# Float32 pair products as three one-pass products of 12-bit parts, with the bank scaled between the second and the third

## The chip, the cores and the metric

One core of one Trainium2 chip. The metric is the device time of one execution in microseconds (us), as the median of several runs; lower is better. Engines are named as in the profile: PE is TensorE, PEld its weight loads, DVE VectorE, ACT ScalarE, POOL GpSimd. A "pair" is one of the 496 products below; a "bank tile" is its 128 x 1024 float32 result in PSUM.

## The reference

32 fields of 128 numbers for 1024 rows; for each of the 496 pairs of fields i < j, field i is multiplied by the pair's own 128 x 128 matrix and then elementwise by field j:

```python
v_i = inputs[:, I_IDX, :]
v_j = inputs[:, J_IDX, :]
transformed = jnp.einsum('bpd,ped->bpe', v_i, W)   # float32
return transformed * v_j                            # 1024 x 496 x 128
```

The check of results passes kernels whose products are off by about one part in 4000. So "correct" below doesn't tell the precision of two variants apart.

## The kernel before

x is held in SBUF transposed (128 x 1024 a field), the weights stream in chunks of 8 pairs. A pair is two float32 matmuls of 512 columns into one bank tile, then VectorE multiplies by field j into an output tile of two pairs, which a DMA takes away.

```python
for q, (i, j) in enumerate(pairs):
    # ... loads of weight chunk q // WC + 3 and of field j + 3 on ScalarE's queue
    po = ppool.tile([P, BT], F32, tag="po", name=f"po_{q}")          # 4 buffers, all of PSUM
    for h in range(0, BT, HB):                                        # BT = 1024, HB = 512
        nc.tensor.matmul(po[:, h : h + HB], w_sb[q // WC][:, q % WC, :],
                         x_sb[i][:, h : h + HB], start=True, stop=True)
    r = q % OC
    if r == 0:
        ot = opool.tile([P, OC, BT], F32, tag="ot", name=f"ot_{q}")
    # ... the last pairs are cut in halves
    nc.vector.tensor_tensor(ot[:, r, :], po[:, :], x_sb[j][:, :], ALU.mult)
    if r == OC - 1:
        nc.sync.dma_start(out=out_v[:, q - r : q + 1, :], in_=ot[:, :, :])
```

## Time and profile before

| what | value |
|---|---|
| time | 877.84 us, median of 3 (877.59 to 878.51); 877.8 to 878.6 beside each later group of runs |
| TensorE | busy 98%, 1984 records of 0.432 us each: 1.72 us a pair |
| VectorE | busy 69%, 1.225 us a pair |
| ScalarE, GpSimd | no arithmetic |
| DMA | 309.7 MB; 418 to 420 GB/s while x still loads, 343 to 351 after that |

A busy line gives the summed busy time, its share of the span and the number of instructions. A line of the costliest groups gives source line, engine, operation, output <- inputs, shape and count, then busy us and mean ns, then the engine's idle time just before those instructions and what ended it. A timeline line gives start, length, and how many instructions in a row it joins. The ends of matmuls are modelled, so I read spacing from the starts, not from the lengths. The lines themselves are in the prediction.

### The profile page before, as it was taken

What the parts mean: (1) busy time and instruction counts of PE and PEld (TensorE: products, weight loads), DVE (VectorE), ACT (ScalarE), POOL (GpSimd) and SP (SyncE); (2) the same over time, 40 slices, a digit from 0 to 9 for tenths busy, and PEclk for the clock granted to TensorE, in tenths of its full rate; (3) what the DMA queues carried; (4) which work ended last, traced back from release to release, by engine and by line L of the source; (5) the groups of instructions that cost most, each with busy time, mean ns of one, the idle gap of its engine ahead of it and who ended that gap; (6) DMA issues with size and microseconds to landing.
All of it is one profiled execution on the core that took longest, in us unless ns stands there. A gap on an engine that the chain in (4) does not pass through costs nothing.

```text
span 876.1 us, 5490 instructions
## 1 busy us (share of the span) xinstructions
PE 856.6 (98%) x1984; PEld 377.1 (43%) x1984; DVE 606.3 (69%) x498; POOL 0.2 (0%) x4
## 2 busy tenths in 40 slices
PE   8997899999999999999999999999999999999997
PEld 3432344444444444444444444444444444444443
DVE  4744677777777777777777777777777777777775
POOL 0000000000000000000000000000000000000000
PEclk9999999999999999999999999999999999999999
DMA  9999999989898898998988889888898989889877
GB/s 349 421 419 421 421 420 415 357 340 354 333 352 342 338 357 333 349 339 341 353 340 346 339 346 352 339 345 339 351 343 341 346 338 355 342 338 351 329 311 296
DMA packets 81898, 309.69 MB, mean 353 GB/s; under 512 B 5584, under 2 KB 5840, under 8 KB 81872
## 3 DMA queue, kind: packets, MB, share of 16 engines
q1 hardware_dynamic: 68624, 262.16, 75.3%
q10 hardware_dynamic: 13248, 47.19, 15.5%
q8 instruction: 15, 0.25, 0.1%
q14 instruction: 11, 0.09, 0.0%
HBM read 49.28 MB, written 260.05 MB: 353 GB/s over the span
## 4 chain that ended last, share of the span: by engine, by line
PE 88%; DMA 11%; DVE 0%; ACTq 0%; DVEq 0%; issue 0%; SPq 0%
PE po L82 88%; DMA x<-in_xt_dram 6%; DMA out_dram<-ot 3%; DMA w<-in_wt_dram 2%; DVE ot L93 0%; DVE ot L99 0%; DVEq L121 0%; ACTq L61 0%; ACTq L53 0%; DVEq L93 0%; SPq L95 0%
## 5 line engine op out<-in xcount | busy, mean ns | idle before, releaser
L82 PE MATMUL po<-x,w 128*128 128x512 f32 x1984 | 856.6, 594 | 13.9 <-DVE ot L93 9.9
L93 DVE TENSOR_TENSOR ot<-po,x 128x1024 f32<-128x1024 f32 x494 | 603.7, 1225 | 264.7 <-PE po L82 228.1
L82 PEld LDWEIGHTS po<-x,w 128*128 128x128 f32 x1984 | 377.1, 190 | 492.6 <-issue 470.0
L99 DVE TENSOR_TENSOR ot<-po,x 128x512 f32<-128x512 f32 x4 | 2.6, 687 | 0.9 <-PE po L82 0.9
L115 POOL MEMSET const-bfloat16-1.0<- 128x1 bf16 x1 | 0.1, 102 | 0.0
L115 POOL MEMSET const-uint8-127<- 128x1 uint8 x1 | 0.1, 102 | 0.0
L115 POOL MEMSET const-float32-0.0<- 128x1 f32 x1 | 0.1, 99 | 0.2 <-issue 0.2
L115 POOL MEMSET const-float32-1.0<- 128x1 f32 x1 | 0.1, 99 | 0.0
## 6 DMA issues: line engine op xcount, KB each, us to landing
out_dram<-ot SPq DMA_DIRECT2D x247, 1024.0 KB, 4.8
w<-in_wt_dram ACTq DMA_DIRECT2D x61, 512.0 KB, 4.3
x<-in_xt_dram ACTq DMA_DIRECT2D x28, 512.0 KB, 12.8
x<-in_xt_dram SPq DMA_DIRECT2D x4, 256.0 KB, 4.6
x<-in_xt_dram SPq DMA_DIRECT2D x2, 512.0 KB, 8.5
out_dram<-ot SPq DMA_DIRECT2D x4, 256.0 KB, 3.3
w<-in_wt_dram ACTq DMA_DIRECT2D x1, 320.0 KB, 6.3
w<-in_wt_dram ACTq DMA_DIRECT2D x1, 128.0 KB, 3.6
```

The costliest lines, as they stand in the source:

```text
L82: nc.tensor.matmul(po[:, h : h + HB], w_sb[q // WC][:, q % WC, :], x_sb[i][:, h : h + HB], start=True, stop=True,)
L93: nc.vector.tensor_tensor(ot[:, r, :], po[:, :], x_sb[j][:, :], ALU.mult)
L99: nc.vector.tensor_tensor(ot[:, r, s], po[:, s], x_sb[j][:, s], ALU.mult)
L115: nc = _bacc.Bacc("TRN2", target_bir_lowering=False, num_devices=1)
```

## The change

The intent: by the Trainium skill, "FP8 and Floating Point Precision", TensorE Precision Notes, a float32 product passes the array four times, and reduced-precision float32 is cut to a short format; I took float32r for that type, and to pass once. Split both operands into an upper and a lower part of 12 bits: w = wh + wl, x = xh + e xl, with e = 2^-12. Four part products are then needed, but Karatsuba's identity makes three of them do, all accumulated in one bank:

    (1 + e) (wh xh + wl xl) + (wl - e wh)(xh - xl) = (wh + wl)(xh + e xl)

The first two products (called F, four matmuls of 512 columns) go in; ScalarE scales the bank by 1 + e in PSUM; the third (S, two matmuls) is added. ScalarE also rounds the upper parts, GpSimd makes the lower parts and the differences. The pairs are walked in another order so that x can load as it goes; the first 15 pairs stay float32. The core of the diff:

```diff
-WC = 8
-OC = 2
+WC = 4
+EPS = 2.0**-12
+NATIVE = 5
+LAG = 2
...
-    return [(i, j) for j in range(1, NF) for i in range(j)]
+    return [(i, j) for i in range(NF - 2, -1, -1) for j in range(i + 1, NF)]
...
+    def split_w(c):
+        raw = w_raw[c].rearrange("p q e -> p (q e)")
+        h, l, d = [wpool.tile([P, WC * P], F32R, tag=t, name=f"{t}_{c}") for t in ("wh", "wl", "wd")]
+        hs = tpool.tile([P, WC * P], F32, tag="t", name=f"whs_{c}")
+        nc.scalar.mul(h, raw, 1.0 - 2.0**-13)
+        nc.gpsimd.tensor_tensor(l, raw, h.bitcast(F32), ALU.subtract)
+        nc.gpsimd.tensor_scalar(hs, h.bitcast(F32), EPS, 1.0, ALU.mult, ALU.mult)
+        nc.gpsimd.tensor_tensor(d, l.bitcast(F32), hs, ALU.subtract)
+    # ... split_x(f): the same for one field, in two halves of 512 columns
...
+    def second(q):
+        r = slice(q % WC * P, (q % WC + 1) * P)
+        for h in range(0, BT, HB):
+            nc.tensor.matmul(po[q][:, h : h + HB], w_s[q // WC][2][:, r], x_s[i][2][:, h : h + HB],
+                             start=False, stop=True, skip_group_check=True)
+    for q in range(NQ + LAG):
+        # ... loads, split_w two chunks ahead, split_x one field ahead
+        # ... the first 15 pairs: two float32 matmuls, as before; all others:
+        for t in (0, 1):
+            for h in range(0, BT, HB):
+                nc.tensor.matmul(po[q][:, h : h + HB], w_s[c][t][:, r], x_s[i][t][:, h : h + HB],
+                                 start=t == 0, stop=t == 1)
+        nc.scalar.mul(po[q], po[q], 1.0 + EPS)
+        if q >= LAG:
+            second(q - LAG)      # where q - LAG is a split pair
+            finish(q - LAG)      # VectorE's product and the output DMA
```

The source puts S of a pair two pairs after its F. The program that was built has another order, as the prediction says.

More of the change, by code (lines that the diff above doesn't have):

```diff
@@ L8 @@
 F32 = mybir.dt.float32
+F32R = mybir.dt.float32r
 ALU = mybir.AluOpType
@@ L40 @@
     pairs = _pairs()
+    nchunk = NQ // WC
     xpool = ctx.enter_context(tc.tile_pool(name="x", bufs=1))
-    wpool = ctx.enter_context(tc.tile_pool(name="w", bufs=4))
+    spool = ctx.enter_context(tc.tile_pool(name="xs", bufs=2))
+    rpool = ctx.enter_context(tc.tile_pool(name="wr", bufs=4))
+    wpool = ctx.enter_context(tc.tile_pool(name="ws", bufs=3))
+    tpool = ctx.enter_context(tc.tile_pool(name="tmp", bufs=2))
     opool = ctx.enter_context(tc.tile_pool(name="o", bufs=6))
@@ L47, with load_x @@
     x_sb = {}
-    def load_x(f, eng, pieces=1):
+    def load_x(f, pieces=1):
         x_sb[f] = xpool.tile([P, BT], F32, tag=f"x{f}", name=f"x_{f}")
@@ L52, in load_x @@
         for k in range(pieces):
-            eng.dma_start(out=x_sb[f][:, k * s : (k + 1) * s], in_=xt[:, f, k * s : (k + 1) * s])
-    nchunk = NQ // WC
-    w_sb = {}
+            nc.sync.dma_start(out=x_sb[f][:, k * s : (k + 1) * s], in_=xt[:, f, k * s : (k + 1) * s])
+    w_raw = {}
     def load_w(c, splits=(0, WC)):
-        w_sb[c] = wpool.tile([P, WC, P], F32, tag="w", name=f"w_{c}")
+        w_raw[c] = rpool.tile([P, WC, P], F32, tag="w", name=f"w_{c}")
         for a, b in zip(splits, splits[1:]):
-            nc.scalar.dma_start(out=w_sb[c][:, a:b, :], in_=wt[:, c * WC + a : c * WC + b, :])
@@ L63 @@
-    load_w(0, (0, 1, 3, WC))
-    load_x(0, nc.sync, 2)
-    load_x(1, nc.sync, 2)
-    load_x(2, nc.sync)
+            nc.sync.dma_start(out=w_raw[c][:, a:b, :], in_=wt[:, c * WC + a : c * WC + b, :])
+    w_s = {}
+    def split_w(c):
[6 more added lines that the diff above has]
+        nc.gpsimd.tensor_tensor(d, l.bitcast(F32), hs, ALU.subtract)
+        w_s[c] = (h, l, d)
@@ new lines, with split_x @@
+    x_s = {}
+    def split_x(f):
+        h, l, d = [spool.tile([P, BT], F32R, tag=t, name=f"{t}_{f}") for t in ("xh", "xl", "xd")]
+        for a in range(0, BT, HB):
+            s = slice(a, a + HB)
+            ls = tpool.tile([P, HB], F32, tag="t", name=f"xls_{f}_{a}")
+            nc.scalar.mul(h[:, s], x_sb[f][:, s], 1.0 - 2.0**-13)
+            nc.gpsimd.tensor_tensor(ls, x_sb[f][:, s], h[:, s].bitcast(F32), ALU.subtract)
+            nc.gpsimd.tensor_scalar(l[:, s], ls, 1.0 / EPS, 1.0, ALU.mult, ALU.mult)
+            nc.gpsimd.tensor_tensor(d[:, s], h[:, s].bitcast(F32), l[:, s].bitcast(F32), ALU.subtract)
+        x_s[f] = (h, l, d)
@@ L67 @@
+    nq0 = NATIVE * (NATIVE + 1) // 2
+    c0 = nq0 // WC
+    load_w(0, (0, 1, WC))
+    load_x(NF - 2, 2)
+    load_x(NF - 1, 2)
+    load_x(NF - 3)
     load_w(1)
-    load_x(3, nc.sync)
+    for f in (NF - 4, NF - 5):
+        load_x(f)
     load_w(2)
-    load_x(4, nc.scalar)
-    load_x(5, nc.scalar)
-    out_v = out.rearrange("q e b -> e q b")
-    ot = None
-    for q, (i, j) in enumerate(pairs):
-        if q % WC == 0 and q // WC + 3 < nchunk:
-            load_w(q // WC + 3)
-        if i == 0 and 5 < j + 3 < NF:
-            load_x(j + 3, nc.scalar)
-        po = ppool.tile([P, BT], F32, tag="po", name=f"po_{q}")
+    out_v = out.rearrange("q e b -> q e b")
@@ new lines, with finish @@
+    po = {}
+    def finish(q):
+        j = pairs[q][1]
+        ot = opool.tile([P, BT], F32, tag="ot", name=f"ot_{q}")
+        pieces = 2 if q >= NQ - 2 else 1
+        s0 = BT // pieces
+        for k in range(pieces):
+            s = slice(k * s0, (k + 1) * s0)
+            nc.vector.tensor_tensor(ot[:, s], po[q][:, s], x_sb[j][:, s], ALU.mult)
+            nc.sync.dma_start(out=out_v[q, :, s], in_=ot[:, s])
+    def second(q):
+        i, _ = pairs[q]
+        r = slice(q % WC * P, (q % WC + 1) * P)
@@ L81 @@
         for h in range(0, BT, HB):
             nc.tensor.matmul(
-                po[:, h : h + HB],
-                w_sb[q // WC][:, q % WC, :],
-                x_sb[i][:, h : h + HB],
-                start=True,
-                stop=True,
-            )
-        r = q % OC
-        if r == 0:
-            ot = opool.tile([P, OC, BT], F32, tag="ot", name=f"ot_{q}")
-        if q < NQ - OC:
-            nc.vector.tensor_tensor(ot[:, r, :], po[:, :], x_sb[j][:, :], ALU.mult)
-            if r == OC - 1:
-                nc.sync.dma_start(out=out_v[:, q - r : q + 1, :], in_=ot[:, :, :])
-        else:
-            for h in range(0, BT, HB):
-                s = slice(h, h + HB)
-                nc.vector.tensor_tensor(ot[:, r, s], po[:, s], x_sb[j][:, s], ALU.mult)
-                nc.sync.dma_start(out=out_v[:, q, s], in_=ot[:, r, s])
+                po[q][:, h : h + HB], w_s[q // WC][2][:, r], x_s[i][2][:, h : h + HB], start=False, stop=True,
@@ new lines, in second @@
+                skip_group_check=True,
+            )
+    for q in range(NQ + LAG):
+        if q < NQ:
+            i, j = pairs[q]
+            c = q // WC
+            if q % WC == 0:
+                if c + 3 < nchunk:
+                    load_w(c + 3)
+                for k in ([c + 2] if c > 0 else [0, 1, 2]):
+                    if c0 <= k < nchunk:
+                        split_w(k)
+            if j == i + 1:
+                for f in ([i - 4] if i < NF - 2 else [NF - 6]):
+                    if f >= 0:
+                        load_x(f)
+                if 0 <= i - 1 < NF - 1 - NATIVE:
+                    split_x(i - 1)
+            po[q] = ppool.tile([P, BT], F32, tag="po", name=f"po_{q}")
+            if q < nq0:
+                for h in range(0, BT, HB):
+                    nc.tensor.matmul(
+                        po[q][:, h : h + HB],
+                        w_raw[c][:, q % WC, :],
+                        x_sb[i][:, h : h + HB],
+                        start=True,
+                        stop=True,
+                    )
+            else:
+                r = slice(q % WC * P, (q % WC + 1) * P)
+                for t in (0, 1):
+                    for h in range(0, BT, HB):
+                        nc.tensor.matmul(
+                            po[q][:, h : h + HB],
+                            w_s[c][t][:, r],
+                            x_s[i][t][:, h : h + HB],
+                            start=t == 0,
+                            stop=t == 1,
+                        )
+                nc.scalar.mul(po[q], po[q], 1.0 + EPS)
+        if q >= LAG:
+            if q - LAG >= nq0:
+                second(q - LAG)
+            finish(q - LAG)
```

## The prediction

> **What bounds the kernel now.** I read the page first (busy shares, chain, costliest groups), then a table of stretches for the load by stage, then timelines of TensorE. The lines of the page:
>
> ```profile
> PE 856.6 (98%) x1984; PEld 377.1 (43%) x1984; DVE 606.3 (69%) x498; POOL 0.2 (0%) x4
> ...
> PE po L82 88%; DMA x<-in_xt_dram 6%; DMA out_dram<-ot 3%; DMA w<-in_wt_dram 2%; DVE ot L93 0%; DVE ot L99 0%; DVEq L121 0%; ACTq L61 0%; ACTq L53 0%; DVEq L93 0%; SPq L95 0%
> ...
> L82 PE MATMUL po<-x,w 128*128 128x512 f32 x1984 | 856.6, 594 | 13.9 <-DVE ot L93 9.9
> L93 DVE TENSOR_TENSOR ot<-po,x 128x1024 f32<-128x1024 f32 x494 | 603.7, 1225 | 264.7 <-PE po L82 228.1
> ```
>
> The chain of work that ended last is TensorE for 88%. There are 496 pairs and 1984 matmul records, four to a pair (two for each half of 512 columns). 856.6/1984 = 0.432 us each, so a pair costs 1.72 us of TensorE. VectorE needs 1.225 us a pair and waits 228 us for TensorE: it has room. Two stretches of the table (columns: us, busy PE, PEld, DVE, POOL with counts, clock, DMA share, GB/s):
>
> ```profile
> 22.00:44.00 22.00, 22.00 (x53) 9.80 (x52) 15.90 (x13) 0.00 (x0) 1.00 1.03 420
> 400.00:500.00 100.00, 100.00 (x235) 44.27 (x234) 71.34 (x59) 0.00 (x0) 1.00 0.89 343
> ```
>
> From 22 to 150 us, while x is still being loaded, the DMA engines give 418 to 420 GB/s at a share of 1.02 to 1.03: this is their ceiling. Later TensorE is always busy and DMA moves 343 to 351. So the kernel is TensorE bound with DMA close behind. The timeline of TensorE in the saturated stage shows what restarting costs:
>
> ```profile
> 68.60 3.70 PE L82 MATMUL po<-x,w 128*128 128x512 f32 x8 [1.08 <-DVE ot L93]
> 73.48 3.70 PE L82 MATMUL po<-x,w 128*128 128x512 f32 x8 [1.18 <-DVE ot L93]
> ```
>
> Eight matmuls without a stop would be 7 x 0.429 + 0.592 = 3.59 us; after a wait they take 3.70, so each wait of TensorE costs about 0.11 us more (the weights' load is then not hidden).
>
> **What the Trainium skill says.** (1) "FP8 and Floating Point Precision", TensorE Precision Notes: true FP32 is four passes through the array, reduced-precision FP32 reads four bytes and is cut to a shorter format. The trace agrees with four if one record is two passes. (2) "TensorE: Matmul & The Clock Gate", Back-to-back issue gap: 512 columns warm take 512/2.4 + 2.5 = 216 ns; half of the traced 0.43 us is 0.215, which agrees. No run yet shows a float32r pass, so 0.216 us is an estimate. (3) "ScalarE: Activation LUTs", What ACT_TABLE_LOAD costs: an ACTIVATE with immediates takes 186 ns + 0.833 ns per element, back-to-back ones overlap by 93 ns. ScalarE computes nothing in this trace, so nothing here confirms it. (4) "GPSIMD Engine Reference", Performance versus the Vector engine: tensor_tensor of 2048 fp32 is 4497 ns there, so about 1.12 us for 512 (estimate); one-input operations are near line rate, I take 0.6 us. GpSimd does no such work in this trace.
>
> **The change, part by part.**
>
> *Removed:* for 481 of 496 pairs the four records of 0.43 us. The first 15 stay as they were: 15 x 1.72 = 25.8 us.
>
> *Added on TensorE:* six one-pass matmuls a pair: F = h and l products, 4 x 0.216 = 0.86 us; S = the difference product, 2 x 0.216 = 0.43 us. Sum 1.29 us, 25% less. If only this counted, 481 x 1.29 = 620 us, and DMA would bind: 309.7 MB / 420 GB/s = 737 us.
>
> *Added between F and S:* ScalarE scales the bank in place, A = 186 + 0.833 x 1024 = 1.04 us. S(q) cannot start before A(q) has ended. The source puts S two pairs after F, which would give A(q) 0.43 + 0.86 + 0.43 + 0.86 = 2.58 us. But the order of instructions in the built kernel is another one. In 102 of the 120 groups of four pairs TensorE's queue stands as F0 F1 S0 F2 S1 F3 S2 S3, then F0 of the next group: only F1 stands between F0 and S0, and only S2 between F3 and S3. ScalarE's queue has the split of a weight chunk (512 elements, 0.61 us) between A2 and A3. TensorE's queue is in order, so it waits.
>
> I walk one group, in us from the start of F0, with 0.20 from the end of a matmul's issue to a reader's start (in the trace VectorE starts 0.63 us after its last matmul's start, whose slot is 0.43), 0.04 back to TensorE (the trace restarts it 0.05 after VectorE), and 0.11 for a restart:
> - F0 0 to 0.86; A0 1.06 to 2.10; F1 to 1.72; S0 could go at 1.72 but waits to 2.14, and with the restart runs 2.25 to 2.68.
> - A1 2.01 to 3.05; F2 2.68 to 3.54; S1 follows at once, to 3.97. A2 3.74 to 4.78; F3 3.97 to 4.83; S2 just fits, 4.83 to 5.26.
> - The weight split takes ScalarE from 4.69 to 5.30; A3 5.21 to 6.25; S3 waits from 5.26 to 6.29 and runs 6.40 to 6.83.
>
> So a group takes 6.83 us instead of 5.16: 1.71 us a pair, which is what a pair costs now. The TensorE time saved is given back as two waits for ScalarE in each group. 120.25 groups x 6.83 = 821 us. In 12 boundaries the next F comes ahead of S3, saving both waits (1.14 + 0.53 us): -20 us. Some 11 groups have S directly behind its own F, about +1.3 us each: +14 us. That leaves 815 us.
>
> *Moved or added beside other work:* the weight split on GpSimd is 2 x 1.12 + 0.6 = 2.85 us a chunk, the x split 5.7 us for each i: 121 x 2.85 + 26 x 5.7 = 493 us, off the path with two chunks of lead. ScalarE: 481 x 0.95 + 173 x 0.52 = 547 us. VectorE stays at 1.225 a pair (610 us). All DMA goes through one queue, with w in 2 KB pieces a partition; at 1.71 us a pair output and weights are 0.59 MB / 1.71 = 345 GB/s, as now. The x loads, now early and saturating, spread over the whole run.
>
> *Ends:* first matmul at about 4.5 us, tail as now 876.1 - 870.5 = 5.6 us. Sum: 4.5 + 25.8 + 815 + 5.6 = 851, plus about 2 from span to time: 853 us. I take 848, because the waits for ScalarE may be a little shorter than I walk them, and every 0.05 us there, paid twice in each of 120 groups, is 12 us in all.
>
> **Rivals.**
> 1. *DMA becomes the bound.* If TensorE does not wait as I think, the floor is 737 us at 420 GB/s, and some 750 to 775 us with the ends and 2 KB pieces. For it: the gap between 343 and 420 GB/s is small, and 1.29 us is less than 0.59 MB / 420 GB/s = 1.40 us. Against it: the built order, which puts S too close to F.
> 2. *ScalarE's round trip is longer than I think.* If A with its semaphores is 0.15 us longer, S0 and S3 wait that much more and S1 and S2 begin to wait too, with two more restarts: 120 x (0.30 + 0.15 + 0.35) = +96 us, some 940 us. For it: S2 fits with only 0.01 us in hand. Against it: where S1 and S2 wait, the later waits shrink in part, so less than this.
> 3. *GpSimd becomes the bound in the first groups.* A group of i with n pairs needs 5.7 + 0.71 n us of GpSimd against 1.71 n of TensorE: equal at 6 pairs, the first split group. If its operations are half again as slow, groups up to about 13 pairs are bound by it: some +15 us.
> 4. *A float32r matmul is no faster than one record of now* (0.43 us): 481 x 2.59 = 1246 us. I give it 4%.
>
> **Range and chances.** The walk of one group gives 1.71 us with perhaps 0.09 either way, which is 43 us; DMA cannot let it fall below 750. I say 848 us, 8 times in 10 within 790 to 905. Faster by over 2% is below 860, slower is above 895: 0.61 faster, 0.26 within, 0.13 slower.
>
> **What the changed profile would show.** Right: matmuls of half the spacing (0.215 us); TensorE's largest wait is for the scaling line of ScalarE, about 1.6 us in each group of four pairs, 180 us or so in all, at the S line; scaling records near 1.04 us; DMA around 350 to 370 GB/s with a share below 0.95 in the middle; VectorE idle between pairs. Wrong: DMA at 415 to 420 throughout with VectorE waiting for output buffers (rival 1); S1 and S2 waiting as well (rival 2); waits for GpSimd before 150 us (rival 3); spacing of 0.43 us (rival 4). A clock granted below 1.00 because TensorE has gaps would also upset it.

## The result, and the profile after

| | before | after |
|---|---|---|
| time, median | 878.17 us (877.59 to 878.66, 4 runs) | 897.87 us (897.74 to 899.2, 4 runs) |
| span, granted clock | 876.1 us, 0.998 | 896.0 us, 0.999 |
| TensorE busy | 98% | 85% |
| DMA at 400 to 500 us | 343 GB/s, share 0.89 | 340 GB/s, share 0.90 |

The ratio is 1.0228 (95% interval 1.021 to 1.0246): slower by 2.3%. I had forecast 848 us and faster. The time lies inside my range, the direction is the one that I had given 0.13.

Lines of the page after, from the busy times and the costliest groups:

```profile
PE 761.1 (85%) x2946; PEld 526.2 (59%) x2946; DVE 607.0 (68%) x498; ACT 558.2 (62%) x655; POOL 549.5 (61%) x523
...
L177 ACT ACTIVATE po<-po 128x1024 f32<-128x1024 f32 x481 | 476.9, 1009 | 298.5 <-PE po L170 298.5
L135 PE MATMUL po<-xd,wd 128*128 128x512 f32 x962 | 325.7, 420 | 123.8 <-ACT po L177 123.0
...
L170 PE MATMUL po<-xh,wh 128*128 128x512 f32 x962 | 300.9, 394 | 0.0
L170 PE MATMUL po<-xl,wl 128*128 128x512 f32 x962 | 298.1, 391 | 0.0
L170 PEld LDWEIGHTS po<-xl,wl 128*128 128x128 f32 x962 | 180.6, 188 | 42.2
```

L170 is F, L177 the scaling, L135 is S. No engine is busy for more than 85%, for F no wait is recorded, and S waits 123 us for the scaling. The list of waits (waiter <- releaser: us in total, times, longest) has it on both halves of TensorE, and the table of stretches shows that DMA is no limit (us, busy PE, PEld, DVE, ACT, POOL with counts, clock, DMA share, GB/s):

```profile
PEld po L135 <- ACT po L177: 162.8, 195, 1.7
...
PE po L135 <- ACT po L177: 123.0, 245, 1.2
```

```profile
400.00:500.00 100.00, 84.48 (x333) 59.05 (x333) 67.52 (x57) 63.49 (x74) 59.14 (x57) 1.00 0.90 340
```

One group of four pairs on TensorE's timeline, from S0 (508.14) to the S0 of the next group (515.15):

```profile
508.14 0.70 PE L135 MATMUL po<-xd,wd 128*128 128x512 f32 x2
508.67 0.63 PE L170 MATMUL po<-xh,wh 128*128 128x512 f32 x2
509.14 0.62 PE L170 MATMUL po<-xl,wl 128*128 128x512 f32 x2
509.60 0.62 PE L135 MATMUL po<-xd,wd 128*128 128x512 f32 x2
510.06 0.63 PE L170 MATMUL po<-xh,wh 128*128 128x512 f32 x2
510.52 0.62 PE L170 MATMUL po<-xl,wl 128*128 128x512 f32 x2
510.98 0.63 PE L135 MATMUL po<-xd,wd 128*128 128x512 f32 x2
512.31 0.73 PE L135 MATMUL po<-xd,wd 128*128 128x512 f32 x2 [0.70 <-ACT po L177]
512.88 0.63 PE L170 MATMUL po<-xh,wh 128*128 128x512 f32 x2
513.35 0.62 PE L170 MATMUL po<-xl,wl 128*128 128x512 f32 x2
513.80 0.62 PE L170 MATMUL po<-xh,wh 128*128 128x512 f32 x2
514.27 0.63 PE L170 MATMUL po<-xl,wl 128*128 128x512 f32 x2
515.15 0.70 PE L135 MATMUL po<-xd,wd 128*128 128x512 f32 x2 [0.26 <-ACT po L177]
```

The order is the predicted one: S0, F2, S1, F3, S2, S3, then F0 and F1 of the next group, and S0 again. Two things are to be seen. A line without a wait starts 0.46 us after the one before it: two matmuls, so **0.230 us a matmul**, where I had put 0.216. And there are two stops: S3 starts 1.33 us after S2 instead of 0.46, and S0 starts 0.88 us after the line before it. What ended the two waits is on ScalarE's timeline (A0 to A3 are the scalings of the four pairs of a group, L86 is the rounding of a weight chunk):

```profile
509.80 1.01 ACT L177 ACTIVATE po<-po 128x1024 f32<-128x1024 f32 x1 [0.50 <-PE po L170]
510.72 0.63 ACT L86 ACTIVATE wh<-w 128x512 fp32r<-128x512 f32 x1
511.24 1.02 ACT L177 ACTIVATE po<-po 128x1024 f32<-128x1024 f32 x1
514.00 1.94 ACT L177 ACTIVATE po<-po 128x1024 f32<-128x1024 f32 x2 [1.75 <-PE po L170]
```

A3 runs 511.24 to 512.26 and S3 starts at 512.31. In the walk of the 119 group starts, the regular group is 7.02 us (median), 11 groups are 5.6 to 5.7 us, and 27 are more than 0.3 us over the median, 15 of them by less than 1 us. The page's chain of waits (TensorE 32%, ScalarE 25%, no releaser 19%, GpSimd 11%) is of little help here. For 93 of S's weight loads the list of waits names GpSimd (67 us in all), but in the trace each of them stands right behind a wait for ScalarE's semaphore. The first two experiments keep all of GpSimd's work, have 5 us and nothing of these waits, and are far faster, so GpSimd isn't the bound.

### The profile page after: what moved, and what is told of

Read it like the earlier page. It is cut to its first block, busy times and chain, and to the rows that moved or that the text cites. A ratio compares the mean times of both kernels' runs of the same rounds, so it can differ in the third digit from the quotient of the medians.

```text
span 896.0 us, 10407 instructions
## 1 busy us (share of the span) xinstructions
PE 761.1 (85%) x2946; PEld 526.2 (59%) x2946; DVE 607.0 (68%) x498; ACT 558.2 (62%) x655; POOL 549.5 (61%) x523
## 4 chain that ended last, share of the span: by engine, by line
PE 32%; ACT 25%; issue 19%; POOL 11%; DMA 1%; DVE 0%; POOLq 0%; ACTq 0%; DVEq 0%
ACT po L177 20%; PE po L170 17%; PE po L135 14%; ACT wh L86 4%; POOL wl L87 4%; POOL wd L89 4%; POOL whs L88 2%; DMA out_dram<-ot 1%; ACT xh L100 1%; POOL xls L101 1%; DVE ot L128 0%; POOL xl L102 0%; POOLq L87 0%; ACTq L177 0%; POOL xd L103 0%
## 5 line engine op out<-in xcount | busy, mean ns | idle before, releaser
L128 DVE TENSOR_TENSOR ot<-po,x 128x1024 f32<-128x1024 f32 (+1 forms) x498 | 607.0, 1220 | 285.4 <-ACT po L177 141.7
L177 ACT ACTIVATE po<-po 128x1024 f32<-128x1024 f32 x481 | 476.9, 1009 | 298.5 <-PE po L170 298.5
L135 PE MATMUL po<-xd,wd 128*128 128x512 f32 x962 | 325.7, 420 | 123.8 <-ACT po L177 123.0
L135 PEld LDWEIGHTS po<-xd,wd 128*128 128x128 f32 x962 | 152.7, 188 | 257.5 <-ACT po L177 162.8
L170 PE MATMUL po<-xh,wh 128*128 128x512 f32 x962 | 300.9, 394 | 0.0
L170 PE MATMUL po<-xl,wl 128*128 128x512 f32 x962 | 298.1, 391 | 0.0
L170 PEld LDWEIGHTS po<-xl,wl 128*128 128x128 f32 x962 | 180.6, 188 | 42.2
L170 PEld LDWEIGHTS po<-xh,wh 128*128 128x128 f32 x962 | 180.6, 188 | 42.1 <-issue 0.5
L89 POOL TENSOR_TENSOR wd<-wl,whs 128x512 fp32r<-128x512 f32 x121 | 156.6, 1294 | 7.9
L86 ACT ACTIVATE wh<-w 128x512 fp32r<-128x512 f32 x121 | 75.5, 624 | 19.3 <-DMA w<-in_wt_dram 19.3
L159 PE MATMUL po<-x,w 128*128 128x512 f32 x60 | 29.6, 656 | 6.2 <-DMA x<-in_xt_dram 6.2
L159 PEld LDWEIGHTS po<-x,w 128*128 128x128 f32 x60 | 12.3, 209 | 22.6 <-issue 21.6
```

The lines of the kernel that those rows point to most:

```text
L86: nc.scalar.mul(h, raw, 1.0 - 2.0**-13)
L89: nc.gpsimd.tensor_tensor(d, l.bitcast(F32), hs, ALU.subtract)
L128: nc.vector.tensor_tensor(ot[:, s], po[q][:, s], x_sb[j][:, s], ALU.mult)
L135: nc.tensor.matmul(po[q][:, h : h + HB], w_s[q // WC][2][:, r], x_s[i][2][:, h : h + HB], start=False, stop=True, skip_group_check=True,)
L159: nc.tensor.matmul(po[q][:, h : h + HB], w_raw[c][:, q % WC, :], x_sb[i][:, h : h + HB], start=True, stop=True,)
L170: nc.tensor.matmul(po[q][:, h : h + HB], w_s[c][t][:, r], x_s[i][t][:, h : h + HB], start=t == 0, stop=t == 1,)
```

## The experiments

The theory after the result: TensorE is bound by ScalarE's round trip as predicted, and the loss against my number comes from sizes (float32r's slot; the boundaries between groups; the start). The rivals: the extra work of ScalarE, GpSimd or DMA slows everything, or the time is ruled by something other than the two waits.

### Is the wait the cause?

**x1_no_scale**: the scaling is left out, wrong by about 2^-12. The built order then puts S right behind its own F.

```diff
-                nc.scalar.mul(po[q], po[q], 1.0 + EPS)
```

> The scaling of the bank by ScalarE is left out and nothing else of the source (wrong on purpose: the h*h and l*l parts lack the factor 1+2^-12, an error of about 1 in 4000). The built order then has S directly behind its own F. Theory (waits for ScalarE between F and S cost about 1.7 us a pair minus 1.387): TensorE needs 6 x 0.231 = 1.39 us a pair, so DMA with 0.59 MB a pair at 420 GB/s = 1.40 us takes over: 750 to 785 us. Rival A (the single DMA queue is already the bound at 92% share): stays above 870 us. Rival B (GpSimd's splits are the bound, as the chain's 11% says): they are unchanged here, so above 860 us.

Measured 770.87 us, ratio 0.878 (0.8767 to 0.8793). Its middle stretch:

```profile
400.00:500.00 100.00, 94.72 (x396) 72.65 (x395) 80.40 (x67) 12.90 (x21) 72.11 (x69) 1.00 1.02 405
```

The scaling and its wait are worth 127 us. Without them DMA is at a share of 1.02 and 405 GB/s: the next bound. GpSimd's work is all there.

**x2_order_lag2** and **x3_order_lag1**: the scaling stays and nothing else changes, but TensorE's instructions are kept in the order of the source: S two pairs behind its F (x2), or one pair (x3, LAG = 1).

```diff
-            nc.tensor.matmul(
+            tc.keep_in_program_order(nc.tensor.matmul(      # for F and for S
```

> TensorE's instructions are kept in the order of the source, so that S(q) always stands behind F(q+2); all else as in the changed kernel, results right. Theory (the built order, not the scaling, is what costs): waits of TensorE for ScalarE at S vanish, but with four banks F(q+2) then waits for VectorE to free the bank of q-2: 0.20 + 1.225 + 0.05 = 1.475 against 0.925 + 0.463 = 1.387 between, so some 0.09 + 0.11 us a pair: 1.59 us a pair, about 800 to 815 us. Rivals A and B: 880 to 900 us, no change.

> The same with S(q) always behind F(q+1), one pair later instead of two; results right. Theory: from the end of F(q) to S(q) TensorE has S(q-1) and F(q+1), 1.387 us, and ScalarE needs 0.20 + 1.01 + 0.04 = 1.25 us, so it never waits except where a split stands in ScalarE's queue (0.15 to 0.4 us a group of four); DMA or TensorE at 1.40 to 1.50 us a pair: 755 to 790 us. Rivals A and B: 880 to 900 us.

Measured 780.32 us (0.8884; 0.8866 to 0.8903) and 782.21 us (0.8906; 0.8888 to 0.8925). All the arithmetic of the change is there, and only the order differs: 117 us. (For x2 I had put 800 to 815 us, too slow.) So the time of the changed kernel is the built order's waits, and nothing that the added work costs elsewhere. With two pairs of distance S never waits, but a bank tile is held for longer and F waits for VectorE to free one. In the waits of x2:

```profile
PEld po L170 <- DVE ot L128: 131.8, 422, 1.3
```

That wait is mostly hidden: x2 is 9 us from x1, which has DMA for its bound as well.

**x4_three_products**: the plain way to use three products: h h + l h + h l with l l left out. No scaling, no difference parts, two fifths of GpSimd's work; the upper parts are rounded without the factor 1 - 2^-13, and LAG is 0.

```diff
-                for t in (0, 1):
+                for n, (tw, tx) in enumerate(((0, 0), (1, 0), (0, 1))):
...
-                nc.scalar.mul(po[q], po[q], 1.0 + EPS)
```

> Three one-pass products without any scaling between: h*h + l*h + h*l, the l*l product dropped (an error of about 2^-24 of the products, as fp32 rounding itself), so ScalarE does not touch the bank and GpSimd makes only l. Results right within rounding. Theory: TensorE 1.39 us a pair in one accumulation, DMA takes over: 750 to 780 us, DMA at 415 to 420 GB/s for long stretches. Rival A: above 870 us. Rival B: also fast, since GpSimd's work falls to 223 us.

Measured 770.11 us, ratio 0.8767 (0.8754 to 0.878): with x1 the fastest of all, 12% below the kernel before and 14% below the changed one. By the algebra it leaves out a term of about 2^-24 of the product; I did not measure its precision apart from passing the check. Stretch:

```profile
400.00:500.00 100.00, 95.01 (x397) 72.69 (x396) 80.83 (x67) 12.68 (x21) 27.50 (x22) 1.00 1.03 408
```

Taking away 60% of GpSimd's work against x1 (72.11 to 27.50 us in the stretch) moved nothing.

### How long is a one-pass matmul?

**x5_bf16_look** and **x6_n256_look**: x1 with bf16 parts (wrong in the last digits), and x1 with matmuls of 256 columns. One run each, of unknown state; I use the spacing only.

```diff
-F32R = mybir.dt.float32r
+F32R = mybir.dt.bfloat16
```

```diff
-        for h in range(0, BT, HB):
+        for h in range(0, BT, MB):      # MB = 256
```

> The kernel without scaling again, but with all parts in bfloat16 instead of float32r (wrong on purpose, in the third digit), to read the slot of a one-pass matmul of 512 columns in unbroken runs. In the changed kernel it is 0.231 us where I had taken 0.216. If the extra 0.015 us belongs to float32r (its weights' load or four-byte reads), bfloat16 shows 0.213 to 0.217 us; if it belongs to any one-pass matmul with its own weights' load on this core, bfloat16 shows 0.229 to 0.232 us too.

> The kernel without scaling, with float32r matmuls of 256 columns instead of 512, twice as many (correct but for the missing scale). If each matmul has a fixed 0.018 us on top of its columns at 2.4 per ns, the slot is 0.107 + 0.018 = 0.125 us and twelve of them take 1.50 us a pair; if a matmul cannot start until the 0.188 us of its own weights' load have passed, the slot is 0.19 us or more and a pair takes 2.3 us or more (about 1150 us in all); if columns simply stream slower (0.451 ns each), it is 0.116 us, 1.39 us a pair and some 770 us.

Times 770.74 and 782.29 us. In x5, lines of two matmuls start 0.43 to 0.44 us apart: 0.2155 us each, which is the 216 ns that the Trainium skill has for 512 columns ("TensorE: Matmul & The Clock Gate", Back-to-back issue gap). In x6, lines of four start 0.48 us apart: 0.120 us each. Both are x1 but for one thing, and in x1 the float32r matmul of 512 columns takes 0.227 us (median), a little less than the 0.230 of the profile after; why isn't shown. So float32r costs more than the page's 216 ns. From x6 to x1, 256 columns more cost 0.107 us, 0.418 ns a column, and 0.013 us a matmul is left: two points and no more, but nearest to the theory of a fixed cost (put at 0.018), since slower columns alone would give 0.1135 us in x6. By shape, the weight loads of x5 are

```profile
L135 PEld LDWEIGHTS <-wd 128*128 128x128 bf16 x962 | 94.4, 98 | 114.7 <-issue 1.6 <-POOL whs L88 0.3
```

98 ns, against 188 ns with float32r in the profile after. The Trainium skill, "TensorE: Matmul & The Clock Gate", Weight-path perf modes, has a fast weight load for types other than FP32, measured there at about twice the speed; the two traces agree, and put float32r with FP32, whose loads took 190 ns in the kernel before. Whether the longer load is what makes the slot longer isn't shown: at 256 columns the slot of 0.120 us is less than the 0.19 us of a load, so the records of loads overlap there.

### What rules the round trip?

**x7_half_scale**: the scaling in two halves of 512 columns, so that the first might start while F's second half still runs.

```diff
-                nc.scalar.mul(po[q], po[q], 1.0 + EPS)
+                for h in range(0, BT, HB):
+                    nc.scalar.mul(po[q][:, h : h + HB], po[q][:, h : h + HB], 1.0 + EPS)
```

> The scaling is issued as two instructions of 512 columns instead of one of 1024, so that S of the first half can start when its half is scaled; the built order changes a little with it (in most groups the two halves of S3 stand on either side of the next F0). Results right. Theory (what costs is the time from F's end to S's start behind too short a stretch of other matmuls): the half is scaled 0.61 us after its F half instead of 1.01, S0 no longer waits and S3 waits 0.2 to 0.5 us instead of 0.9: 5.55 + 0.5 + 0.1 = 6.1 us a group, 780 to 815 us. If ScalarE's total busy time were the limit instead (it rises by some 0.2 us a pair), the time would stay at 890 us or grow.

Measured 934.83 us, ratio 1.0645 (1.0629 to 1.0661): a clear miss in the other direction. The half scaling and a piece of ScalarE's and TensorE's timelines:

```profile
L178 ACT ACTIVATE po<-po 128x512 f32<-128x512 f32 x962 | 544.8, 580 | 270.4 <-PE po L170 258.7
```

```profile
500.99 1.20 ACT L178 ACTIVATE po<-po 128x512 f32<-128x512 f32 x2 [1.51 <-PE po L170]
```

```profile
499.86 0.62 PE L170 MATMUL po<-xh,wh 128*128 128x512 f32 x2
500.32 0.63 PE L170 MATMUL po<-xl,wl 128*128 128x512 f32 x2
500.79 0.39 PE L135 MATMUL po<-xd,wd 128*128 128x512 f32 x1
502.32 0.70 PE L135 MATMUL po<-xd,wd 128*128 128x512 f32 x2 [1.15 <-ACT po L178]
```

The first half of F's second product starts at 500.32, the second 0.23 us later, and ScalarE starts at 500.99: as late as for the whole bank tile. S starts at 502.32, after both halves have ended (502.19). So in this build the waits are for the whole tile, and two halves take 1.20 us where the whole takes 1.01. But TensorE's built order moved as well: in most groups the next F0 stands between the two halves of S3. The regular group grows from 7.02 to 7.21 us, which is 23 of the 37 us lost; 12 us more lie in the irregular groups and 2 us in the start. So how much the longer round trip alone costs, this run can't say.

**x8_wh_on_gpsimd**: the rounding of the weight chunk, which stands ahead of A3 on ScalarE, goes to GpSimd.

```diff
-        nc.scalar.mul(h, raw, 1.0 - 2.0**-13)
+        nc.gpsimd.tensor_scalar(h, raw, 1.0 - 2.0**-13, 1.0, ALU.mult, ALU.mult)
```

> The rounding of the weight chunk goes from ScalarE to GpSimd (0.62 us more a chunk there), so nothing stands in ScalarE's queue between A2 and A3. Results right. In the built order 112 group boundaries instead of 102 now have both waits. Theory: S3 waits 0.25 to 0.3 us less in each group, -33 us, and ten more waiting boundaries cost 10 x 1.4 = +14 us: about 879 us (865 to 890). If the delay by the split never reaches S3, there is no gain and 900 to 912 us follow.

Measured 898.57 us, ratio 1.0232 (1.0215 to 1.0249): no gain in the whole. The group starts say why. The regular group did shrink, from 7.02 to 6.93 us, so the rounding ahead of A3 costs 0.09 us and not the 0.18 of my walk. But the built order moved as well. In 113 groups instead of 102, S3 now stands between S2 and the next F0: of the short groups (5.6 us, 11 in the changed kernel) one is left. 119 x 0.09 = 10.7 us gained, and as much lost.

### Is DMA's 405 GB/s to be raised in the fast version?

**x9_three_w8**, **x10_three_w8_two_queues**, **x11_three_w8_loads_apart**: x4 with weight chunks of 8 pairs (4 KB pieces, as before the change); then the weight loads on ScalarE's queue; then x loads there too.

```diff
-WC = 4
+WC = 8                                                      # x9; buffers and lead made to fit
-            nc.sync.dma_start(out=w_raw[c][:, a:b, :], ...)
+            nc.scalar.dma_start(out=w_raw[c][:, a:b, :], ...)   # x10
-            nc.sync.dma_start(out=x_sb[f][:, k * s : (k + 1) * s], ...)
+            nc.scalar.dma_start(out=x_sb[f][:, k * s : (k + 1) * s], ...)   # x11
```

> The three products without scaling (results right to rounding), with the weights loaded in chunks of eight pairs, so 4 KB a partition in one piece as in the kernel before instead of 2 KB. The kernels without the wait stand at 770 us with DMA at 403 to 410 GB/s, where the kernel before reached 418 to 420 with 4 KB pieces. If the 2 KB pieces cost that, 309.7 MB / 420 GB/s = 737 plus about 12 us of ends: 748 to 758 us. If something else sets 405 GB/s (one queue, or output without gaps), it stays at 766 to 772 us.

> As the one before, with the weights' loads issued from ScalarE's queue instead of sharing the one queue with x and the output. If one shared queue holds DMA back (the loads wait in it behind output), 3 to 10 us less than the run before; if the DMA engines themselves are the limit, the same within 3 us.

> As the one before, with the x loads on ScalarE's queue as well, so that the output has its queue alone as in the kernel before. x is then no longer held back by the output in the queue and comes as early as ScalarE's own order lets it. Same two theories: within 3 us of the run before if the engines are the limit.

Measured 773.88, 793.22 and 778.63 us (0.8821, 0.9026, 0.8868). None beats x4. Neither the piece size nor the single queue makes the difference between 405 and the 420 GB/s of the kernel before. But the two figures are of different stages: the kernel before had its 420 while x was loading, and there the fast kernels have it too (x1 417 GB/s from 22 to 44 us, x11 417 from 30 to 130 us). Why the rate is lower in the later stage, where by the issues some 86% of the bytes are output instead of 59 to 74%, stays open. In x10 the granted clock of the profiled run was 0.973, and its DMA rate fell to 387 in the middle; why is not settled either. At 405 GB/s the 309.7 MB take 765 us (an estimate), so x4 is within 1% of that bound.

### Which term of the sum was off?

**x12_group_order**: TensorE's order is pinned to F0 F1 S0 F2 S1 F3 S2 S3 in all 120 groups, so that no boundary is irregular.

```diff
+            for p in ((), (q - 1,), (q - 1,), (q - 1, q))[q % WC] if q >= nq0 else ():
+                second(p)
+                finish(p)                     # F and S kept in program order
```

> The changed kernel with TensorE's order pinned to F0 F1 S0 F2 S1 F3 S2 S3 in all 120 groups, the order that I walked in the prediction (results right); the weight split now stands behind A0 in ScalarE's queue, where it delays nobody. From the changed kernel's trace (regular group 7.02 us) a group should take 6.96: 35.2 to the first split pair + 120.25 x 6.96 = 837 + 7 of ends = 879 us, plus what the x splits in ScalarE's queue cost, 26 times 0.3 to 0.5 us: 887 to 893 us. If the irregular boundaries of the built order were what made it slow, 15 us or more below 887.

Measured 886.33 us, ratio 1.0096 (1.0077 to 1.0114), just under the 887 to 893 that I had put, and level with the kernel before within 2%. The regular group is 6.93 us: in this build the weight rounding stands behind A3 and delays nobody. From the first F (33.64) to the last S (877.23 + 0.46) it takes 844.0 us, of which 120.25 x 6.93 = 833.3 are regular. Of the other 10.7 us, 9 come before 135 us. There the waits for GpSimd, my third rival, are to be seen: TensorE's matmuls wait 3.9 us for it in all. The worst is one of 2.77 us that ends at 62.7 us on the timeline, after which the granted clock was 0.57 from 63 to 67 us (some 1.7 us lost, an estimate).

**x13_group_order_bf16**: x12 with bf16 parts, wrong in the last digits: only what float32r itself costs is taken away. **x15_built_order_bf16**: the same with the changed kernel in its own order.

```diff
-F32R = mybir.dt.float32r
+F32R = mybir.dt.bfloat16
-        nc.gpsimd.tensor_tensor(l, raw, h.bitcast(F32), ALU.subtract)
+        nc.gpsimd.tensor_tensor(l, raw, h, ALU.subtract)           # and so on
```

> The same pinned order with all parts in bfloat16 (wrong on purpose beyond the third digit), whose slot is 0.2155 us where float32r has 0.230. 18 slots of a group lie on its path (F0, S0, F2, S1, F3, S3), so 18 x 0.0145 = 0.26 us less a group, 31 us in all, if the slot is the term that I mis-sized; up to 0.2 us a group more where its separate weights' load no longer waits with the matmul. So 834 to 862 us. If the slot is not on the path, the same as the float32r run.

> The changed kernel in its own built order, with bf16 parts in place of float32r (wrong on purpose in the last digits): only what float32r itself costs TensorE is taken away. Theory (the slot of 0.230 instead of 0.2155 us and the load exposed after a wait are the mis-sized terms; between the ordered kernels they were worth 0.53 us a group): 898 - 120 x 0.50 to 0.53 = 832 to 842 us, a group of 6.45 to 6.55 us, and so near the 848 that I forecast. Rival (the loss comes from the irregular boundaries, the late start and ScalarE's own queue, and a faster slot only makes TensorE wait longer for ScalarE): 875 to 895 us, the group still above 6.85.

Measured 826.19 us (0.9399; 0.938 to 0.9418), 60 us under x12, and 844.96 us (0.9623; 0.9607 to 0.9639), 53 us under the changed kernel: a bit more and a bit less than expected. From S3 to the next S3, first x12 and then x13:

```profile
599.79 0.73 PE L135 MATMUL po<-xd,wd 128*128 128x512 f32 x2 [0.63 <-ACT po L177]
600.36 0.62 PE L170 MATMUL po<-xh,wh 128*128 128x512 f32 x2
600.83 0.62 PE L170 MATMUL po<-xl,wl 128*128 128x512 f32 x2
...
606.72 0.73 PE L135 MATMUL po<-xd,wd 128*128 128x512 f32 x2 [0.63 <-ACT po L177]
```

```profile
607.48 0.59 PE L135 MATMUL po<-xd,wd 128*128 128x512 bf16 x2 [0.66 <-ACT po L177]
607.91 0.59 PE L170 MATMUL po<-xh,wh 128*128 128x512 bf16 x2
608.34 0.59 PE L170 MATMUL po<-xl,wl 128*128 128x512 bf16 x2
...
613.87 0.59 PE L135 MATMUL po<-xd,wd 128*128 128x512 bf16 x2 [0.66 <-ACT po L177]
```

It is 6.93 us in x12 and 6.39 us in x13 (6.40 in its median group): 0.53 us less. 18 matmul slots of a group lie on the path between its two waits and each is 0.0145 us shorter: 0.26. The rest is the restart. At S3, 0.57 us pass with float32r from S to the next line instead of 0.46, and with bf16 the usual 0.43: 0.11. At S0 (medians of all groups) the float32r matmul starts 0.14 us after its scaling has ended and the next line comes 0.08 us late; the bf16 one starts after 0.05 us and nothing is late: 0.17. Together that is 0.54. So with bf16 a restart costs nothing. The waits agree: in the profile after, the weight load of S itself waits 162.8 us for the scaling; in x15 the idle time ahead of those loads has no releaser in the profile, and only the matmul waits for ScalarE. The list of waits of x15:

```profile
PEld L135 <- issue: 211.7, 278, 1.6
...
PE po L135 <- ACT po L177: 135.1, 244, 1.3
```

The recorded order of TensorE in x15 is that of the changed kernel, with 58 of 2946 records missing from the trace. Its regular group is 6.55 us (median) where the pinned order has 6.40: the weight rounding ahead of A3 again, 0.15 us with the shorter slots. So float32r's own cost, slot and restart, decides the sign here: with bf16's the same order is 3.8% faster than the kernel before, with float32r's 2.3% slower.

**x14_group_order_x_gpsimd**: x12 with the rounding of x, the other guest in ScalarE's queue, on GpSimd.

```diff
-            nc.scalar.mul(h[:, s], x_sb[f][:, s], 1.0 - 2.0**-13)
+            nc.gpsimd.tensor_scalar(h[:, s], x_sb[f][:, s], 1.0 - 2.0**-13, 1.0, ALU.mult, ALU.mult)
```

> The pinned order in float32r with the rounding of x moved from ScalarE to GpSimd, so that ScalarE has only bank scalings and the weight split (results right). If the x splits between two scalings cost 0.3 to 0.5 us each of 26 times two, 8 to 14 us below the pinned float32r run; if they hide, the same within 2 us; if GpSimd (1.24 us more for each x) becomes late in the first groups, above it.

Measured 883.32 us, ratio 1.0054 (1.0037 to 1.007): 3 us under x12 instead of 8 to 14. The regular group stays at 6.93 us. ScalarE's rounding of x costs little.

## Why the prediction was wrong

The mechanism was right, and was shown by x1, x2 and x3: the built order puts S0 one F behind its own and S3 behind S2, and TensorE gives its gain back in two waits for the scaling in each group. In the profile after F never waits, S1 and S2 do not wait in regular groups, DMA stays at 340 GB/s with a share of 0.90, VectorE has room, the clock is 0.999. What was wrong is the sum, in four terms that all went one way:

| term | put at | measured | off by |
|---|---|---|---|
| start of the first split pair (4.5 + 25.8) | 30.3 | 35.2 | +4.9 |
| 120.25 regular groups | 6.83 each: 821 | 7.02 each: 844.2 | +23.2 |
| all other boundaries (-20 + 14) | -6 | +11.4 | +17.4 |
| after the last S, and from span to time (5.6 + 2) | 7.6 | 7.1 | -0.5 |
| taken off because the waits "may be a little shorter" | -5 | 0 | +5 |
| sum | 848 | 897.9 | +50 |

The measured 11.4 is what is left between 35.2 and the end of the last S (890.3 + 0.46) after the regular groups.

**The first step that failed** is "six one-pass matmuls a pair: F = h and l products, 4 x 0.216 = 0.86 us; S = the difference product, 2 x 0.216". I had said there that no run yet showed a float32r pass. It takes 0.230 us. A group of 12 lines of two matmuls is 12 x 0.4615 = 5.54 us and not 5.16, 0.38 more. The two waits with their restarts are 7.02 - 5.54 = 1.48 us and not 6.83 - 5.16 = 1.67, 0.19 less: ScalarE runs through a part of the longer slots, and A3 is held up by the weight rounding for 0.09 and not 0.18 us. So the group came out 0.19 long. Walked again with 0.2308 us a slot and every other figure as I had it, my group comes to 7.02 us, the measured one: for the group the slot is the whole miss. (The scaling takes 1.009 us and not 1.04, but S0's later start makes up for that.) With bf16, whose slot is the one I had put, the same order has 6.55 us a group and 845 us in all (x15); there is no restart to pay there, so the agreement with 848 is partly luck, since the boundaries below were off by much the same.

**The second** is "In 12 boundaries the next F comes ahead of S3 ... -20 us. Some 11 groups have S directly behind its own F, about +1.3 us each: +14 us". The short groups save 1.4 us each, 15.4 for 11 of them and not 20. In nine of them the group behind is 7.5 to 7.7 us, so some 0.6 us of each is given back, which I had not walked. (My 102 groups are those whose S3 stands between S2 and the next F0. Exactly as I walked them stand 81 of 119.) The groups of 8.3 to 8.35 us (1.3 more) are there as I put them; the first groups of the run and some of 7.9 us come on top. Long groups together cost 26.6 us. x8, with one short group left, is the control: its regular group gains 0.09 us, and its time doesn't move.

**The third** is the start. The first eight records stand about 0.85 us apart where later ones stand 0.43 apart, 3.4 us more, and between the fourth and the fifth TensorE waited 1.60 us for x. The trace before has the slow records too, its first six (3.95 to 9.12 us), so I could have read this term there.

**The rivals.** The second (a longer round trip) was closest in its time, 940, but not in its way: S1 and S2 do not wait, and the round trip itself was about what I had: with the restart 1.37 us at S3 and 1.43 at S0, where I had 1.39. The third (GpSimd in the first groups) is real but small: 3.9 us of waits in x12. The first (DMA at once) is what happens when the waits are gone: 770 to 782 us at 391 to 411 GB/s (stretches of 100 us from 100 to 700 us), lower than the 420 I had put. The fourth (0.43 us a pass) didn't happen.

**The chances.** I gave faster 0.61 though three terms stood on estimates that no trace had shown, and shaded the sum down by 5 us. A slot 7% longer alone (0.19 us a group in the walk) moves the forecast to about 871 us, inside 2% of before; the boundaries take it past 880.

## What to carry to other kernels

Where one engine's product goes to a second engine and back to the first, look at the built order and not at the source: 117 us of 898 lay in the order of TensorE's instructions alone, with every operation kept. Ask also whether the round trip is needed: three plain products without the term of 2^-24 need neither the scaling nor the differences, and ran in 770 us (their precision was not measured). And when a forecast rests on a duration that no trace of the case shows, such as a new data type's slot, widen for it, because it is multiplied by every instruction of the kernel.

## What the Trainium skill lacked or had wrong

- "TensorE: Matmul & The Clock Gate", Back-to-back issue gap: 216 ns for 512 columns holds for bf16 here (0.2155 us in x5 and x13). For float32r it is 0.227 us in x1 and 0.230 in the profile after, and 0.120 us for 256 columns. The page makes no difference between the types. Its other figure for a stream of loads and matmuls, about 131 ns at 512 columns, was seen in no run.
- The same page, on weight loads: 98 ns for bf16 and 188 ns for float32r. That a float32r matmul that waited restarts 0.11 us late and a bf16 one doesn't (0.57 to 0.46 us, and 0.43 to 0.43) is on no page that I read.
- "GPSIMD Engine Reference", Performance versus the Vector engine: a quarter of its 4497 ns for 2048 elements is 1.12 us; 512 elements took 1.28 to 1.30 us in the float32r kernels, and 1.15 to 1.16 us in the bf16 one (x5). Operations with one input, near line rate by the page's Engine selection, took 0.62 us.
- "ScalarE: Activation LUTs", What ACT_TABLE_LOAD costs: 1024 elements would take 1.039 us; from PSUM to PSUM they took 1.009 us, and a back-to-back pair 1.93 us, so 0.09 us of overlap, as the page has it (93 ns).
- "DMA: Bandwidth & Descriptors", Where 436 GB/s comes from: it says that about 358 GB/s bind between HBM and SBUF and 435 elsewhere. One core alone moved 418 to 420 GB/s in the kernel before and 391 to 411 in x1 to x4, both between HBM and SBUF. So that sentence doesn't hold for one core alone, for which the same page's table of measured transfers has up to 425.
